# One metaformer layer on one core: the width transform, the filters and the mixing in tiles of 64 rows by 128 columns

## The chip, the core and the metric

The kernel runs on one core of a Trainium2 chip. A core has TensorE (PE: matrix products into PSUM, with weight loads of their own, PEld), VectorE (DVE), ScalarE (ACT), GpSimd (POOL) and SyncE (SP), each with its own queue of instructions in a fixed order, and 16 DMA engines that all queues share. PSUM has eight banks of 128 x 512 float32. The metric is the device time of one execution in microseconds; times are compared as medians of several executions.

## The reference

The input x is 8 images of 128 x 128 pixels with 96 channels, all float32. The layer computes, for each image:

```python
z  = layernorm_over_channels(x)
p  = relu(z @ w1.T) ** 2                       # 192 channels (scale 1, bias 0 as parameters)
f  = rfft2(p)                                  # 128 x 65 complex, per channel
r  = softmax(mlp(mean(z), mean(relu(bn(z @ sp_w.T)))))      # 3 x 192 weights per image
c  = sum(r[s] * resized_filter[s] for s in range(3))        # complex, 128 x 65 x 192
x  = x + irfft2(f * c) @ w2.T                  # back to 96 channels
y  = q(relu(q(q8(layernorm(x)) @ q8(W1).T + b1))) ; out = x + q(q8(y) @ q8(W2).T + b2)
```

q8 rounds to an 8-bit float with 2 bits of mantissa (float8e5), q to a 16-bit one. The three learned filters are small (16x9, 8x4, 24x13) and are resized to 128x65 by cubic interpolation, which is a product with fixed matrices. The Fourier transforms are products with fixed cosine and sine matrices too.

## The kernel before

Each image passes three **streams** of work, for which the kernel has one function each.

*before* (stream "a") works on units of four image columns. It normalises, projects (line 825, `px`), rectifies and squares on ScalarE, transforms along the height (line 854, `py`), folds rows that mirror each other (line 866) and stores the result Y to DRAM. At the end of an image a short chain (`rate_v0` to `rate_n`) gives the softmax weights.

*spectrum* (stream "s") works on 33 groups `g` of four rows of the half-transformed image (the last ones have fewer). A group's 192 channels are handled as three parts `q` of 64; two rows `k` of it lie beside each other. Its steps:

- `load_y` and `load_t` (SP's queue) bring Y as `yt` and the stored, half-resized filters T as `tb`; `weigh` (line 1028, GpSimd) multiplies `tb` in place by the softmax weights.
- `along_w` (line 1038) transforms along the width. Its float32 products have 64 rows of weights (`yt`) and 64 columns of them, and stream the 65 columns of the constant F2. Four of them, one for each quarter of the 128 x 128 array, follow each other: two halves `i` of the rows and two `k` of the columns.
- `filters_of` (line 1055) makes the filters in the same way, streaming the 130 columns of RW.
- `copy_sr` (line 1071), `make` (1078), `times` (1084 and 1089) and `turn_back` (1098 and 1101) form the complex product on ScalarE, VectorE and GpSimd and leave it in `xf`.
- For each pair `p` of groups, `mix_low` and `mix` (line 1136, both through `mix_part`) multiply `xf` with w2, streaming 96 columns into `pv`. The upper half of the odd columns uses a negated copy, w2N. `mixed` (line 1155) copies one part of `pv` to a tile B, `combine` (lines 1169 and 1171) adds it to, or takes the rest of `pv` from it, giving V. `invert` (line 1177) transforms back along the width, `inverted` copies and `store_v` stores.

*after* (stream "c") works on blocks of 16 image columns in units of four. `load_v` (lines 1267 and 1268, SP's queue) brings x and V as `t` and `vin`; `last` (line 1273) transforms back along the height; `residual` and `measure` add and take statistics on VectorE. `quantise` normalises one column at a time to float8 in the tile z8, on ScalarE (line 1297) and for one column in eight on VectorE (line 1295); in the last image every second column goes to VectorE. `turn` (line 1302) transposes four columns by a product with an 8-bit identity; `turned` casts the result to float8, on ScalarE (line 1316), in the last image on VectorE (line 1314). `first` (1320), `accumulated` (1327), `biased` (1331), `hidden` (1340, partly 1338), `second` (1347), `put` (1358), `bias` (1362) and `add_up` (1365) are the two layers of the feed-forward network.

A float32 matmul shows in the profile as two records of MATMUL and two of LDWEIGHTS. Products of the line set that the planner calls QUARTER (`along_w`, `filters_of`, `mix_low`, `mix`) leave the array's full-size mode.

**The order of the work.** Nothing runs in the order in which it is written. Each step is entered with `at(...)`: a place in time, what it needs, and the PSUM banks that it takes. `in_order` (line 395) then plays a list schedule on five engines: among the steps that are able to run on an engine it takes the one with the lowest score, which is its place (from the tables WINDOWS and OFFSETS) plus PATIENCE times its delay, and for TensorE plus TURN if the step would change between quarter and full mode. Durations are the fixed table COST (line 157). Six of the eight PSUM banks are dealt out by this plan. The resulting order is written into all queues and holds as it is.

Of the kernel before, what the change touches and what calls it, by code (L numbers as in the profile page):

```python
# [43 lines left out]
MED = 192  # L44
# [11 lines left out]
NG = 31  # L56
# [4 lines left out]
QW = 4  # L61
NQ = WB // QW
# [6 lines left out]
    "a": ((-200.9, 193.5), (639.2, 783.6), (807.7, 922.4), (818.6, 80.5), (148.2, 908), (1102.5, 495.5), (1851.5, 145.6), (2347.7, 470.5)),  # L69
    "s": ((676.9, 253), (431.2, 1046), (911.9, 290.8), (986.6, 574), (-10.7, 261.5), (686.4, 714.9), (1669.9, 93.5), (1887.9, 399.6)),  # L70
    "c": ((1205.2, 777.7), (1178.4, 353), (1360.1, 364.5), (2329.6, 155.8), (2330.5, 482.5), (2472.9, 753.3), (2695.6, 163.1), (2430.1, 646.2)),
}
OFFSETS = {
    "a_context": 98.12,
    "a_fold": 75.91,
    "a_inverse": -202.76,
    "a_load_r": -32.82,
    "a_load_x": -65.67,
    "a_load_xT": 129.83,
    "a_measure": 6.73,  # L80
    "a_project": 64.92,
    "a_put": -0.36,
    "a_rate_e": -236.48,
    "a_rate_n": 287.05,
    "a_rate_p0": -429.86,
    "a_rate_p1": 10.66,
    "a_rate_p2": -69.53,
    "a_rate_v0": -132.22,
    "a_rate_v1": 71.89,
    "a_rate_v2": -99.13,  # L90
    "a_rate_v3": -109.42,
    "a_rectify": -39.91,
    "a_rest": 0.92,
    "a_root": -123.7,
    "a_scale": -16.84,
    "a_square": 71.92,
    "a_store_r": 43.88,
    "a_store_y": -293.45,
    "a_transform": -53,
    "a_variance": 83.26,  # L100
    "c_accumulated": -93.43,
    "c_add_up": -46.53,
    "c_bias": -6.84,
    "c_biased": -64.47,
    "c_first": 13.27,
    "c_hidden": -20.41,
    "c_hidden_2": -145.18,
    "c_hidden_v": -14.93,
    "c_inverse": -0.79,
    "c_last": -164.24,  # L110
    "c_load_v": 67,
    "c_measure": 187.47,
    "c_put8": 23.31,
    "c_quantise": 188.57,
    "c_quantise_v": 329.63,
    "c_residual": -27.11,
    "c_rest": -161.76,
    "c_root": 97.28,
    "c_second": -234.45,
    "c_store": 15.78,  # L120
    "c_turn8": -593.06,
    "c_turned8": 183.6,
    "c_turned8_v": 3.41,
    "c_variance": -133.82,
    "s_alone_t": 91.08,
    "s_alone_x": 250.65,
    "s_alone_z": 38.64,
    "s_along_w": -51.21,
    "s_combine": -13.92,
    "s_copy_sr": -135.74,  # L130
    "s_filters_of": 34.27,
    "s_invert": -8.66,
    "s_inverted": -204.05,
    "s_load_t": 114.08,
    "s_load_y": 112.07,
    "s_make": 78.5,
    "s_mix": 85.47,
    "s_mix_low": 17.63,
    "s_mixed": -265.36,
    "s_store_v": -66.27,  # L140
    "s_times": -169.22,
    "s_turn_back": 36.2,
    "s_weigh": 4.83,
}
WAIT, PATIENCE, TURN = (0, 0, 0, 0, 1.42), (1.06, 54.4, 7.19, 78.2, 48.3), 5100.78
# [52 lines left out]
    "c_turned8_v": (DVE, 0.68, 0),  # L198
    "c_hidden_v": (DVE, 0.6, 0),
# [40 lines left out]
SHARED = {"a_scale", "c_biased", "a_rate_n", "a_rate_v3"}  # L240
# [154 lines left out]
def in_order(ops):  # L395
# [5 lines left out]

    n = len(ops)
# [15 lines left out]
    quarter, shared = [k in QUARTER for k in kinds], [k in SHARED for k in kinds]  # L418

# [14 lines left out]
    while len(order) < n:  # L434
        for e in stale:
# [4 lines left out]
            for i in able[e]:  # L440
                if e == PE:
                    t = last[PE] - (MODES[2] if mode and quarter[i] else MODES[1] if mode != quarter[i] else MODES[0])
                elif e == ACT and queued[i]:
                    t = max(issue, begun + 0.05)
                else:
                    t = last[e] - OVERLAP[e]
                if e == ACT and issue > t:
                    t = issue
                t = max(t, ready[i])
                if ops[i].banks:  # L450
                    if len(open_banks) < ops[i].banks:
                        continue
                    t = max(t, open_banks[ops[i].banks - 1])
                found.append((t, i))
# [29 lines left out]
        if e == PE:  # L484
            mode = quarter[i]
        if moves[i] > 0:
# [28 lines left out]
def metaformer_kernel(ctx: ExitStack, tc: tile.TileContext, a: dict, out: bass.AP):  # L515
# [49 lines left out]
    ident8 = const.tile([128, 128], F8, name="ident8")  # L565
    ones = const.tile([128, 1], F32, name="ones")
# [15 lines left out]
    w2N = const.tile([128, 3, C], F32, name="w2N")  # L582
# [6 lines left out]
    def projection(sp):  # L589
# [3 lines left out]
        ident = sp.tile([128, 128], F32, name="ident")  # L593
# [32 lines left out]
        def others():  # L626
            for i in range(2):
                nc.sync.dma_start(out=w2C[64 * i : 64 * i + 64, :, :], in_=a["w2T"].rearrange("(q m) c -> m q c", q=3))
            nc.vector.tensor_scalar(w2N, w2C, -1.0, None, ALU.mult)
# [367 lines left out]
    def spectrum(b, t0, P):  # L997
# [17 lines left out]
        def load_t(g):  # L1015
            tb = kept["tb", g] = psp.tile([128, 2 * MED], F32, name="tb", tag="tb", bufs=3)
# [9 lines left out]
        def weigh(g):  # L1026
            p = slice(0, 128 if g <= NG else 64)
            nc.gpsimd.tensor_tensor(kept["tb", g][p, :], kept["tb", g][p, :], rates[b][p, :], ALU.mult)  # L1028

        def along_w(g):  # L1030
            halves = [bank("pz") for _ in range(2)]
            kept["pz", g] = halves
            for cs in range(2 if g <= NG else 1):
                for q in range(3):
                    for k in range(2):
                        for i in range(2):
                            rows, c = slice(64 * i, 64 * i + 64), 2 * q + (cs if i == 0 else 1 - cs)
                            nc.tensor.matmul(  # L1038
                                halves[i][64 * k : 64 * k + 64, c * L : (c + 1) * L],
                                lhsT=kept["yt", g][rows, cs, q, k, :],  # L1040
                                rhs=F2[rows, cs, :],
                                start=True,
                                stop=True,
                            )

        def filters_of(g):
            pf = kept["pf", g] = psz.tile([128, 2, 512], F32, name="pf", tag="pf")
            tb = kept.pop(("tb", g))

            for q in range(3):  # L1050
                for k in range(2):
                    m0 = k * MED + 64 * q
                    for s in range(2 if g <= NG else 1):
                        p = slice(64 * s, 64 * s + 64)
                        nc.tensor.matmul(  # L1055
                            pf[64 * k : 64 * k + 64, s, q * 2 * L : (q + 1) * 2 * L],
                            lhsT=tb[p, m0 : m0 + 64],
                            rhs=RW[p, :],
                            start=True,
                            stop=True,  # L1060
                        )
# [64 lines left out]
        def mix_part(p, columns):  # L1126

            for i in columns:
                for q in range(3):
                    for h in range(2):  # L1130
                        for r in range(2):
                            if i >= len(_columns(p, r)):
                                continue
                            g, k = _columns(p, r)[i]
                            half, rows = slice(64 * h, 64 * h + 64), slice(64 * r, 64 * r + 64)
                            nc.tensor.matmul(  # L1136
                                kept["pv", p, r][half, i * C : (i + 1) * C],
                                lhsT=kept["xf", g][rows, k, q, half],
                                rhs=(w2N if k == 1 and h == 1 else w2C)[rows, q, :],
# [12 lines left out]
        def mixed(p, r):  # L1152
            v = kept["B", p, r] = psp.tile([128, 2 * C], F32, name="B", tag=f"B{r}")
# [9 lines left out]
        def combine(p, r, cs):  # L1163
# [4 lines left out]
            if cs == 0:  # L1168
                nc.vector.tensor_tensor(v, a, b, ALU.add)
            else:  # L1170
                nc.vector.tensor_tensor(v, b, a, ALU.subtract)
# [320 lines left out]
```

## Time and profile before

| | us |
|---|---|
| median of 3 runs (2870.8 to 2886.89) | 2871.54 |
| the profiled execution | 2874.85 |
| its span, first to last instruction | 2873.1 |
| TensorE busy, matmul | 2450.5 |
| VectorE busy | 2305.3 |
| ScalarE busy | 2142.1 |
| GpSimd busy | 1696.3 |

A row of the profile names a line, an engine, an operation, what it writes and reads, the shape and the count, then busy time and the mean of one in ns. "<-" in a row of waits means "was released by". "issue" is time in which an engine waited for nothing that the profile shows. A matmul record has a modelled end: records overlap, so the busy time of a group of them is the union. A queue named "instruction" carries the instructions of an engine.

### The profile page before, as it was taken

The page shows a single profiled execution, that of the slowest core. Times are in us where ns is not written, and L with a number is a line of the kernel's source. Part 1 is how long each engine was busy: PE and PEld are TensorE (multiplying, and loading weights), DVE is VectorE, ACT ScalarE, POOL GpSimd, SP SyncE. Part 2 cuts the span into 40 slices and gives each one's busy share as a digit, 9 for nine tenths or more (in the row PEclk, how much of TensorE's full clock was granted, in tenths as well). Part 3 has the DMA queues.
Part 4 walks back from the last instruction along what each step waited for, and adds up shares of the span by engine and source line. Part 5 has one row for each costly group of instructions (what it writes and reads, how often), then busy time and mean ns, then how long its engine had stood idle before and what let it go on. Part 6 is the DMA issues. An engine that isn't in the chain of part 4 may idle for free.

```text
span 2873.1 us, 98792 instructions
## 1 busy us (share of the span) xinstructions
PE 2450.5 (85%) x40162; PEld 1787.2 (62%) x40162; DVE 2305.3 (80%) x5485; ACT 2142.1 (75%) x4332; POOL 1696.3 (59%) x2534
## 2 busy tenths in 40 slices
PE   5888888988898899999989899898988988788664
PEld 3456666666666666666666667666666665556443
DVE  5568777788878877898988888897887878788697
ACT  2355445687875868878888788787888988889776
POOL 3135544566665555657767656566666676668544
PEclk9789999999999999999999899999999999999775
DMA  7788878987889788789877788778676575655431
GB/s 212 211 278 257 246 229 235 273 238 215 225 238 267 230 230 254 217 267 277 257 221 206 228 240 247 209 225 232 201 215 197 170 229 157 184 163 170 149 110 45
DMA packets 786015, 621.67 MB, mean 216 GB/s; under 512 B 578548, under 2 KB 719916, under 8 KB 785536
## 3 DMA queue, kind: packets, MB, share of 16 engines
q1 hardware_dynamic: 697496, 464.33, 58.5%
q10 hardware_dynamic: 88064, 151.02, 14.7%
q8 instruction: 317, 5.19, 0.7%
q14 instruction: 138, 1.13, 0.1%
HBM read 407.03 MB, written 208.16 MB: 214 GB/s over the span
## 4 chain that ended last, share of the span: by engine, by line
PE 47%; ACT 17%; DVE 12%; issue 8%; DMA 5%; POOL 2%; SPq 1%; ACTq 1%; POOLq 0%; DVEq 0%
PE px L825 8%; PE pv L1136 7%; PE py L854 7%; PE pf L1055 5%; PE pz L1038 5%; ACT y L1327 5%; PE pg L1177 4%; ACT h L1340 4%; PE pk L1273 3%; PE po L1347 3%; PE ph L1320 3%; ACT z L1297 2%; DVE st L737 2%; DMA vin<-Vd 2%; DMA yt<-Yd 2%
## 5 line engine op out<-in xcount | busy, mean ns | idle before, releaser
L825 PE MATMUL px<-W1S,zT 97*128 97x240 f32 x2048 | 508.4, 385 | 48.5 <-DVE zT L812 15.9
L825 PEld LDWEIGHTS px<-W1S,zT 97*128 97x128 f32 x2048 | 393.4, 198 | 158.5 <-issue 34.3
L854 PE MATMUL py<-X,F 128*128 128x384 f32 x1024 | 446.1, 531 | 15.1 <-DVE yst L866 4.8
L1327 ACT CAST y<-ph 128x512 f16<-128x512 f32 x768 | 417.9, 603 | 45.1 <-PE ph L1320 35.7
L1098 POOL TENSOR_TENSOR xf<-t 128x390 f32<-128x390 f32 x256 | 232.4, 908 | 348.7 <-DVE t L1084 337.2
L836 ACT ACTIVATE rl<-px 128x480 f32<-128x480 f32 x512 | 291.1, 579 | 133.1 <-PE px L825 111.4
L1340 ACT ACTIVATE h<-y 128x1536 fp8e5<-128x1536 f16 (+1 forms) x256 | 371.6, 1452 | 22.1 <-DVE y L1331 20.8
L1297 ACT ACTIVATE z<-t,ln_m,ln_r 128x96 fp8e5<-128x96 f32 x848 | 363.0, 475 | 10.5 <-POOL ln_m L770 3.8
L1331 DVE TENSOR_TENSOR y<-y,b1q 128x1536 f16<-128x1536 f16 x256 | 308.3, 1205 | 77.8 <-ACT y L1327 77.1
L850 POOL TENSOR_TENSOR sacc<-sacc,rl 128x192 f32<-128x192 f32 x248 | 176.4, 711 | 303.3 <-ACT rl L836 290.8
L1136 PE MATMUL pv<-w2C,xf 64*64 64x96 f32 x9264 | 317.8, 250 | 41.4 <-issue 40.6
L866 DVE TENSOR_TENSOR yst<-py,yb 128x384 f32<-128x384 f32 x512 | 262.7, 546 | 91.6 <-PE py L854 27.7
L1028 POOL TENSOR_TENSOR tb<-tb,r 128x384 f32<-128x384 f32 (+1 forms) x264 | 296.4, 1123 | 46.3 <-DMA tb<-T 42.2
L1078 DVE TENSOR_TENSOR d<-pz,sr 128x390 f32<-128x390 f32 x512 | 265.1, 553 | 66.5 <-ACT sr L1071 65.7
L1136 PEld LDWEIGHTS pv<-w2C,xf 64*64 64x64 f32 x9264 | 287.9, 137 | 43.2 <-issue 39.0
L1055 PE MATMUL pf<-RW,tb 64*64 64x130 f32 x6240 | 253.5, 288 | 58.9 <-issue 24.9
L1320 PE MATMUL ph<-zT,W1q 96*128 96x512 fp8e5 x768 | 257.5, 415 | 38.6 <-DVE zT L1314 13.6
L1038 PE MATMUL pz<-F,yt 64*64 64x65 f32 x12480 | 257.3, 224 | 34.5 <-issue 23.2
L1084 DVE TENSOR_TENSOR t<-d,pf 128x780 f32<-128x780 f32 x256 | 245.1, 958 | 47.1 <-PE pf L1055 19.0
L1038 PEld LDWEIGHTS pz<-F,yt 64*64 64x64 f32 x12480 | 232.0, 138 | 67.8 <-issue 31.9
L1055 PEld LDWEIGHTS pf<-RW,tb 64*64 64x64 f32 x6240 | 189.5, 139 | 130.0 <-issue 58.9
L1347 PE MATMUL po<-W2q,h 128*128 128x96 fp8e5 x3072 | 194.0, 218 | 81.3 <-ACT h L1340 54.3
(129 smaller groups left out, 5085.8 us busy)
## 6 DMA issues: line engine op xcount, KB each, us to landing
yt<-Yd SPq DMA_DIRECT2D x1040, 96.0 KB
Yd<-yst ACTq DMA_DIRECT2D x256, 384.0 KB
xb<-in_xw SPq DMA_DIRECT2D x64, 768.0 KB
rB<-Rd SPq DMA_DIRECT2D x128, 384.0 KB
zT<-in_xT SPq DMA_DIRECT2D x128, 384.0 KB
tb<-T SPq DMA_DIRECT2D x256, 192.0 KB
Vd<-gst ACTq DMA_DIRECT2D x128, 384.0 KB
t<-in_x SPq DMA_DIRECT2D x64, 768.0 KB
```

The lines of the kernel that those rows point to most:

```text
L825: nc.tensor.matmul(px[:, i * (MED + SCTX) : (i + 1) * (MED + SCTX)], lhsT=zTs[(b * NU // 2 + u // 2) % NZT][:, QW * (u % 2) + i0 + i, :], ...
L836: nc.scalar.activation(kept["rl", u][:, i0 : i0 + 2, :].rearrange("h w m -> h (w m)"), kept.pop(("px", u, i0)), AF.Relu)
L854: nc.tensor.matmul(py, lhsT=F1, rhs=kept["X", u][:, i0 : i0 + 2, :].rearrange("h w m -> h (w m)"), start=True, stop=True)
L1028: nc.gpsimd.tensor_tensor(kept["tb", g][p, :], kept["tb", g][p, :], rates[b][p, :], ALU.mult)
L1038: nc.tensor.matmul(halves[i][64 * k : 64 * k + 64, c * L : (c + 1) * L], lhsT=kept["yt", g][rows, cs, q, k, :], rhs=F2[rows, cs, :], start ...
L1055: nc.tensor.matmul(pf[64 * k : 64 * k + 64, s, q * 2 * L : (q + 1) * 2 * L], lhsT=tb[p, m0 : m0 + 64], rhs=RW[p, :], start=True, stop=True,)
L1136: nc.tensor.matmul(kept["pv", p, r][half, i * C : (i + 1) * C], lhsT=kept["xf", g][rows, k, q, half], rhs=(w2N if k == 1 and h == 1 else w ...
L1297: nc.scalar.activation(z, t, AF.Identity, bias=m, scale=r, saturate=False)
L1320: nc.tensor.matmul(kept["ph", u, n], lhsT=W1q[:, n * 128 : (n + 1) * 128], rhs=kept["zT", u], start=True, stop=True)
L1327: nc.scalar.copy(kept["y", u][:, n, :], kept.pop(("ph", u, n)))
L1331: nc.vector.tensor_tensor(y, y, b1q, ALU.add)
L1340: nc.scalar.activation(h, y, AF.Relu, saturate=False)
```

## The change

The change has four parts.

1. `along_w`, `filters_of` and `mix_part` use weights of 64 rows and 128 columns. One product then covers both rows `k` of a group, or both halves `h`, so each function issues half as many. For this `weigh` writes its product to a new tile `tw` in another order (part `q` outside, row `k` inside). As w2N can't be used for half of the columns of a product, it is dropped; the sign goes into `combine`, which multiplies B by a column of +1 and -1 (`sides`) in a scalar_tensor_tensor.
2. `tb` has two buffers instead of three and is released by `weigh`, `tw` has two, B has one instead of two. The waits follow: `weigh` waits for `filters_of` two groups back, `mixed` and `mix_low` for `combine` of the pair before.
3. In the last two images (EXACT = 6) `quantise` runs on GpSimd for every column and writes float32 into `vin`, whose values are used up by then; `turn` transposes in float32 with a float32 identity, as step `turn32`; `turned` casts to float8 on VectorE. `load_v` waits for `turn32` two blocks back.
4. The planner knows that TensorE's instructions come in blocks of 256: INSTR counts those of each step, and a step that would cross into a block before PAGE (4.5 in its units) after the last crossing is held back in the plan. The tables WINDOWS and OFFSETS have new numbers throughout, and WAIT, PATIENCE and TURN too. COST keeps its numbers and gains two rows.

```diff
+EXACT = 6
...
-WAIT, PATIENCE, TURN = (0, 0, 0, 0, 1.42), (1.06, 54.4, 7.19, 78.2, 48.3), 5100.78
+WAIT, PATIENCE, TURN = (0, 0, 0, 0, 2.2), (1.22, 0.556, 94, 1.87, 44.4), 0.63
...
+    "c_turn32": (PE, 1.06, 0),
+    "c_quantise_p": (POOL, 0.26, 0),
...
-SHARED = {"a_scale", "c_biased", "a_rate_n", "a_rate_v3"}
+SHARED = {"a_scale", "c_biased", "a_rate_n", "a_rate_v3", "c_quantise_v", "c_hidden_v"}
+INSTR = {
+    "a_project": 8, "a_transform": 4, "a_rate_p0": 4, "a_rate_p1": 8, "a_rate_p2": 12, "s_along_w": 48,
+    "s_filters_of": 24, "s_mix_low": 48, "s_mix": 48, "s_invert": 4, "c_last": 4, "c_turn8": 8, "c_turn32": 16,
+    "c_first": 2, "c_second": 24, "_rows": 8, "_ends": 16, "_make_weights": 4,
+}
+PAGE = 4.5
...
+                if e == PE and count[i] + page >= 256:
+                    over = t + (took[i] - MODES[0]) * (256 - page) / count[i]
+                    t += max(0.0, turned + PAGE - over)
                 found.append((t, i))
...
-            nc.gpsimd.tensor_tensor(kept["tb", g][p, :], kept["tb", g][p, :], rates[b][p, :], ALU.mult)
+            tw = kept["tw", g] = psp.tile([128, 2 * MED], F32, name="tw", tag="tw")
+            tb, order = kept.pop(("tb", g)), "p (k q m) -> p k q m"
+            nc.gpsimd.tensor_tensor(
+                tw[p, :].rearrange("p (q k m) -> p k q m", q=3, k=2),
+                tb[p, :].rearrange(order, k=2, q=3),
+                rates[b][p, :].rearrange(order, k=2, q=3),
+                ALU.mult,
+            )
...
-                    for k in range(2):
-                        for i in range(2):
-                            rows, c = slice(64 * i, 64 * i + 64), 2 * q + (cs if i == 0 else 1 - cs)
-                            nc.tensor.matmul(
-                                halves[i][64 * k : 64 * k + 64, c * L : (c + 1) * L],
-                                lhsT=kept["yt", g][rows, cs, q, k, :],
+                    for i in range(2):
+                        rows, c = slice(64 * i, 64 * i + 64), 2 * q + (cs if i == 0 else 1 - cs)
                         nc.tensor.matmul(
+                            halves[i][:, c * L : (c + 1) * L],
+                            lhsT=kept["yt", g][rows, cs, q, :, :].rearrange("w k m -> w (k m)"),
+                            rhs=F2[rows, cs, :],
...
+                    nc.tensor.matmul(
+                        pf[:, s, q * 2 * L : (q + 1) * 2 * L],
+                        lhsT=tw[p, 128 * q : 128 * q + 128],
+                        rhs=RW[p, :],
...
                             nc.tensor.matmul(
-                                kept["pv", p, r][half, i * C : (i + 1) * C],
-                                lhsT=kept["xf", g][rows, k, q, half],
-                                rhs=(w2N if k == 1 and h == 1 else w2C)[rows, q, :],
+                                kept["pv", p, r][:, i * C : (i + 1) * C],
+                                lhsT=kept["xf", g][rows, k, q, :],
+                                rhs=w2C[rows, q, :],
...
-            v = kept["B", p, r] = psp.tile([128, 2 * C], F32, name="B", tag=f"B{r}")
+            v = kept["B", p, r] = psp.tile([128, 2 * C], F32, name="B", tag=f"B{r}", bufs=1)
...
-                nc.vector.tensor_tensor(v, a, b, ALU.add)
+                nc.vector.scalar_tensor_tensor(v, b, sides, a, ALU.mult, ALU.add)
             else:
-                nc.vector.tensor_tensor(v, b, a, ALU.subtract)
+                nc.vector.scalar_tensor_tensor(v, b, sides, a, ALU.mult, ALU.subtract)
...
-            return "quantise_v" if i % 8 == 7 or b == B - 1 and i % 2 == 1 else "quantise"
+            return "quantise_p" if b >= EXACT else "quantise_v" if i % 8 == 7 else "quantise"
...
+            if b >= EXACT:
+                nc.gpsimd.tensor_scalar(z, t, r, m, ALU.mult, ALU.add)
+                return
...
-                    rhs=ident8,
+                    rhs=ident if b >= EXACT else ident8,
...
-            if b == B - 1:
+            if b >= EXACT:
                 nc.vector.tensor_copy(kept["zT", u], pz, saturate=False)
...
-                after = [one("last", blk - 2, n) for n in range(NQ)] + [one("store", blk - 5)]
+                after = [one(k, blk - 2, n) for n in range(NQ) for k in ("last", "turn32")] + [one("store", blk - 5)]
```

## The prediction

> **What bounds the kernel now.** I read the busy shares and the chain of the page first, then the long middle stretch alone, then TensorE's own waits in it, then the order of time around one mixing step.
>
> ```profile
> PE 2450.5 (85%) x40162; PEld 1787.2 (62%) x40162; DVE 2305.3 (80%) x5485; ACT 2142.1 (75%) x4332; POOL 1696.3 (59%) x2534
> ...
> q8 instruction: 317, 5.19, 0.7%
> ...
> PE 47%; ACT 17%; DVE 12%; issue 8%; DMA 5%; POOL 2%; SPq 1%; ACTq 1%; POOLq 0%; DVEq 0%
> ```
>
> No engine is full, but TensorE and "issue" are 55% of the chain. The stretch 360 to 2520 (us, PE busy, PEld, DVE, ACT, POOL, clock, DMA share, GB/s):
>
> ```profile
> 360.00:2520.00 2160.00, 1922.45 (x33949) 1429.73 (x33948) 1784.63 (x4176) 1702.80 (x3477) 1348.41 (x1971) 0.96 0.78 227
> ```
>
> TensorE is busy 89% there. Who let it wait in that stretch:
>
> ```profile
> PE pv L1136 <- issue: 70.9, 38, 4.1
> PE pf L1055 <- issue: 22.5, 17, 4.2
> PE pz L1038 <- issue: 18.5, 11, 3.5
> PE po L1347 <- ACT h L1340: 16.8, 23, 2.1
> ```
>
> With three small rows (4.2, 3.3, 2.8) "issue" is 122 us. So TensorE's work and its missing instructions fill 2045 of 2160 us (95%), and all other engines together cost it 115 us. TensorE is the bound; what happens in lines 1038, 1055 and 1136 counts nearly in full.
>
> The order of time (start, length, what):
>
> ```profile
> 1509.46 0.71 PE L1136 MATMUL pv<-w2C,xf 64*64 64x96 f32 x11 [2.63 <-issue]
> ...
> 1522.66 0.93 PE L1038 MATMUL pz<-F,yt 64*64 64x65 f32 x48
> 1523.41 0.85 PE L1055 MATMUL pf<-RW,tb 64*64 64x130 f32 x24
> 1524.08 1.24 PE L1136 MATMUL pv<-w2C,xf 64*64 64x96 f32 x50
> ```
>
> A float32 matmul is two records. Four records, one per 64x64 quarter, run at once: a **round**. Start to start, line 1038 takes 0.75 us for 12 rounds and line 1055 0.67 for 6; single records give a median round of 58, 111 and 82 ns (65, 130 and 96 columns). The first line is a stall: mixing stands 2.63 us with nothing to wait for but instructions.
>
> [...]
>
> [...]
>
> ```profile
> L932 PEld LDWEIGHTS pm<-sc,fc1b x16: 106/108/109, 209.4 to 2343.0; 48*36 48x36 f32 x16
> L1038 PEld LDWEIGHTS pz<-F,yt x12480: 129/135/228, 235.6 to 2659.0; 64*64 64x64 f32 x199
> L1179 PEld LDWEIGHTS pg<-V,GL x16: 187/190/190, 494.7 to 2674.8; 128*128 128x128 f32 x16
> L1179 PE MATMUL pg<-V,GL x16: 244/260/275, 494.9 to 2674.9; 128*128 128x96 f32 x16
> 1519.20 0.36 PE L1179 MATMUL pg<-V,GL 128*128 128x96 f32 x2
> ```
>
> 36, 64, 128 columns: 108, 135, 190 ns, some 0.85 ns a column over a fixed part. The last two rows are the nearest thing to the new form: two short float32 passes with 128-column weights. The pair takes 0.36 us, the first alone 0.246: the second ends **0.11 us** later, although 96 columns stream in 0.08 (line 1136). The load paces it, not the stream.
>
> [...]
>
> ```profile
> 57.77 0.58 PE L675 MATMUL pt<-cw,rh 24*128 24x384 f32 x1
> 63.99 0.60 PE L675 MATMUL pt<-cw,rh 16*128 16x384 f32 x3
> ```
>
> One takes 0.58 with its load, three at once 0.60: loads of different row groups don't queue.
>
> **The change part by part.**
>
> *Tiles of 64x128.* A call covers both column halves, so calls halve (records: line 1038 12480 to 6240, 1055 6240 to 3120, 1136 12288 to 6144), but a round is now two records, and rounds stay 3120, 1560 and 3072. The streams are unchanged; the weight loads are twice as wide, so a round lasts at least the 111 ns of line 1179. Transform: 3120 x (111 - 58) = +165 us. Filters: 111 already, 0. Mixing: 3072 x (111 - 82) = +89. Together **+254 us**, 87% of it (10838 of 12480 records) between 360 and 2520: +221. Bounds: 0, if the wide load were hidden, which line 1179 speaks against; far more, if the two row groups' loads queued, which line 675 speaks against.
>
> *Instruction blocks.* TensorE issues 2 x 40162 = 80,300 instructions, afterwards 80,300 - 31,000 + 512 = 49,800: some 198 blocks for 317. A mixing round brought 8 instructions in 82 ns (a block in 2.6 us), then 4 in 111 (7.1 us). The longest stalls are about 4 us, so a block will arrive while the one before is used. I take 95% of 122 us away: **-116**, between -60 and -133 (the whole run's sum).
>
> *The middle stretch:* +221 - 116 = +105. With TensorE slower, the 115 us of waits on others shrink; I take 30%, -34. **+71.** *Before 360:* 6% of the rounds, +16, half hidden by 79 us of idle TensorE: **+8**.
>
> *Combining.* The minus sign leaves w2N and goes into line 1169/1171 as a scalar_tensor_tensor: 496 of 346 ns. The nearest row, line 971 with the same 128x192, has a median of 418: 0 to +36 us on VectorE (it has 17% idle)[...]. I take **+10**.
>
> *Buffers.* The weighted filters get their own tile (tw, 2), tb goes from 3 to 2 but is free after weigh: GpSimd's 264 instructions of 1.12 us stay, and its strided write costs 0 to 10% of 296 us on an engine 59% busy: 0. The load instructions are as many as before. B goes from 2 to 1: line 1155 on ScalarE and mix_low on TensorE now wait for the combining of p - 1; queued behind them are all of ScalarE's and TensorE's later work. Cover: 128 pairs in 2420 us are 19 us apart, combining ends some 3 us after mixing. 0; where mixings are bunched, up to 3 us each.
>
> *Batches 6 and 7 (EXACT).* 256 quantisations go to GpSimd: 176 leave ScalarE (x 475 = -84 us), 80 VectorE (x 684 = -55). GpSimd's price isn't shown for 96 columns; between 0.21 us (line 559, 16 columns) and 0.4 (a quarter of line 1098's 390-column 0.91 over its fixed part): I take 0.3, +77. Batch 6's 32 casts move from ScalarE (609) to VectorE (679). Turning in float32: 64 units, 8 passes of 110 ns for 4 of 56: +42 us on TensorE. z8 now lies in vin, so SP's load waits for the turning two blocks back, with filter and y loads behind it; blocks are some 20 us apart there, so 0. After 2700 VectorE is busiest (144 of 173) and loses 0.7 x 8 us a block less the 0 of its casts: -25. From 2330 to 2700 ScalarE is at 88% and TensorE at 81%; TensorE gets 17 + 21, ScalarE loses 73: +15. **-10** together.
>
> *The order.* Leaving a tiling mode cost 5100 in the old scores, 0.63 in the new. TensorE switches 576 times now; entering costs some 0.15 us (197 ns from the last full record's end to the first quarter record's, against 58). I take 40% more, 230 x 0.15 = **+35**, between -40 (its new moments fit the engines better) and +120 (the table still prices transform and mixing as narrow tiles).
>
> Sum: 71 + 8 + 10 - 10 + 35 = +114. The profiled execution took 2874.85 (span 2873.1, 1.75 around it), 3.3 above the median of the runs shown, 2871.54. So 2989 profiled, about **2985** as a median.
>
> **The rivals.**
> 1. *Wide loads hide* (0.07): the round stays at its stream. Then -116, -10, no fewer other waits: about 2760. For it: the load records of line 1136 overlap everything now. Against: there a load (64 columns) is no longer than its stream.
> 2. *Gain and loss cancel* (0.08): the order's waits fall by half and the engines' slack takes the rest: 2845 to 2900.
> 3. *The order misfits* (0.12): planned at 58 ns a round, executed at 111, TensorE arrives late at everything placed after it; the 115 us of waits double: 3080 to 3200.
> 4. *Row groups' loads queue* (0.03): 222 ns a round, 3120 x 164 + 1560 x 111 + 3072 x 140 = +1115: about 3850.
>
> The forecast itself (0.70) has 2905 to 3075. Faster ends where the round stays under about 75 ns for the transform and 90 for mixing.
>
> **How the numbers follow.** The range takes the forecast's own, half of case 2 and the foot of case 3: 2885 to 3090. This kernel's measurement can't tell less than about 1% from no change. Faster by more than that 0.07, within 0.08, slower 0.85.
>
> **What would show it.** Line of along_w: 24 records a group instead of 48, but a length of some 1.5 us for 0.93; mixing some 1.4 a half for 1.0; filters unchanged near 0.85. TensorE's "issue" waits under 20 us, q8 near 200 packets, PE busy above 92% in the middle. Combining at 350 to 420 ns, quantising on GpSimd near 0.3 us. I am wrong if a round of two wide records is much nearer 60 than 111 ns.

## The result, and the profile after

The changed kernel takes 2965.04 us (median of 4 runs, 2959.96 to 2968.79), the kernel before 2871.43 (4 runs, 2870.8 to 2886.89): a ratio of 1.031 with an interval of 1.027 to 1.035, so it is slower by 3.1%. Its profiled execution took 2965.69 us, its span 2963.9. The forecast was 2985, from 2885 to 3090.

The page of the changed kernel: busy shares, the queue of TensorE's instructions (packets, MB, share), and the chain.

```profile
PE 2701.0 (91%) x24914; PEld 2075.7 (70%) x24914; DVE 2333.0 (79%) x5438; ACT 2085.4 (70%) x4124; POOL 1801.3 (61%) x2790
...
q8 instruction: 198, 3.24, 0.5%
...
PE 55%; ACT 11%; DVE 8%; DMA 4%; POOL 3%; issue 2%; SPq 1%; ACTq 0%; POOLq 0%; DVEq 0%
```

TensorE has 38% fewer matmul records and 250.5 us more busy time. Its instructions arrive in 198 packets instead of 317, and "issue" falls from 8% of the chain to 2%. The middle stretch of the changed kernel (columns as before: us, PE, PEld, DVE, ACT, POOL, clock, DMA share, GB/s):

```profile
360.00:2520.00 2160.00, 2071.32 (x20162) 1615.01 (x20162) 1786.76 (x4142) 1685.25 (x3407) 1318.67 (x1951) 0.98 0.78 223
```

TensorE is busy 96% of it, instead of 89%. Its waits over the whole run of the changed kernel, longest sums first (us in total, times, longest):

```profile
PE po L1374 <- ACT h L1367: 65.2, 41, 5.6
PE px L847 <- DVE yst L888: 24.1, 9, 13.9
PE po L1374 <- DVE h L1365: 15.5, 8, 2.5
PE pf L1081 <- POOL xf L1124: 13.8, 17, 1.7
```

No row of them is "issue", which had 134 us in the whole run before. The order of time in the changed kernel (start, length, what):

```profile
1509.07 0.94 PE L1081 MATMUL pf<-RW,tw 64*128 64x130 f32 x12
1509.85 1.45 PE L1066 MATMUL pz<-F,yt 64*128 64x65 f32 x24
...
1513.68 1.58 PE L1160 MATMUL pv<-w2C,xf 64*128 64x96 f32 x24
```

The transform takes 1.45 us for 12 rounds of two records (0.93 before), a mixing half 1.58 (1.24), the filters 0.94 (0.85). Single records give a median of 111 to 112 ns from round to round on all three lines, whether 65, 96 or 130 columns stream.

Three groups of the changed kernel that the prediction priced (busy us, mean ns, idle before with its releaser):

```profile
L1193 DVE SCALAR_TENSOR_TENSOR V<-B,sides,pv 128x192 f32<-128x192 f32 x248 | 101.2, 408 | 104.1 <-ACT B L1179 86.9 <-ACT V L1185 16.9
L1319 POOL TENSOR_SCALAR vin<-t,ln_r,ln_m 128x96 f32<-128x96 f32 x256 | 118.5, 477 | 1.2
L1329 PE MATMUL pz<-ident,vin 128*96 128x128 f32 x512 | 74.5, 293 | 2.7 <-POOL vin L1319 2.2 <-DVE d L1104 0.3
```

And GpSimd's longest waits in the changed kernel; the third is new:

```profile
POOL sacc L872 <- ACT rl L858: 268.1, 115, 19.1
POOL xf L1124 <- DVE t L1110: 224.8, 105, 7.8
POOL tw L1052 <- PE pf L1081: 148.2, 73, 10.8
```

`weigh` now waits 148 us for the filters two groups back.

**Where the time went.** The span is TensorE's busy time plus its idle time. From 2450.5 + 422.6 it went to 2701.0 + 262.9 us: 250.5 more work, 159.7 less idling, 90.8 in all. By phases: 4 us before the first `along_w`, 67 from there to the last mixing, 20 in the tail after the last mixing (202 to 222). That much could be read without another run. It doesn't tell which part of the change is responsible, because the parts came together.

### The profile page after: what moved, and what is told of

The parts are those of the page before. It is cut to its first block, busy times and chain, and to the rows that moved or that the text cites. A ratio compares the mean times of both kernels' runs of the same rounds, so it can differ in the third digit from the quotient of the medians.

```text
span 2963.9 us, 68657 instructions
## 1 busy us (share of the span) xinstructions
PE 2701.0 (91%) x24914; PEld 2075.7 (70%) x24914; DVE 2333.0 (79%) x5438; ACT 2085.4 (70%) x4124; POOL 1801.3 (61%) x2790
## 3 DMA queue, kind: packets, MB, share of 16 engines
q8 instruction: 198, 3.24, 0.5%
## 4 chain that ended last, share of the span: by engine, by line
PE 55%; ACT 11%; DVE 8%; DMA 4%; POOL 3%; issue 2%; SPq 1%; ACTq 0%; POOLq 0%; DVEq 0%
PE pv L1160 10%; PE pz L1066 9%; PE px L847 8%; PE py L876 7%; PE pf L1081 5%; PE pk L1297 4%; PE pg L1201 4%; PE po L1374 3%; PE ph L1347 3%; ACT y L1354 3%; ACT h L1367 2%; DVE y L1358 2%; DMA yt<-Yd 2%; PE pz L1329 2%; ACT z L1324 1%
## 5 line engine op out<-in xcount | busy, mean ns | idle before, releaser
L1066 PE MATMUL pz<-F,yt 64*128 64x65 f32 x6240 | 411.2, 277 | 8.2 <-ACT rl L858 2.8
L1066 PEld LDWEIGHTS pz<-F,yt 64*128 64x128 f32 x6240 | 388.5, 193 | 41.6 <-issue 11.7
L1160 PE MATMUL pv<-w2C,xf 64*128 64x96 f32 x6144 | 405.0, 281 | 3.7 <-POOL xf L1127 2.4
L1358 DVE TENSOR_TENSOR y<-y,b1q 128x1536 f16<-128x1536 f16 x256 | 343.2, 1341 | 67.0 <-ACT y L1354 66.0
L1160 PEld LDWEIGHTS pv<-w2C,xf 64*128 64x128 f32 x6144 | 386.6, 196 | 10.8 <-POOL xf L1127 2.7
L1052 POOL TENSOR_TENSOR tw<-tb,r 128x384 f32<-128x384 f32 (+1 forms) x264 | 285.5, 1083 | 176.3 <-PE pf L1081 148.2
L1324 ACT ACTIVATE z<-t,ln_m,ln_r 128x96 fp8e5<-128x96 f32 x672 | 286.5, 470 | 8.8 <-DMA yt<-Yd 3.3
L1374 PEld LDWEIGHTS <-h 128*128 128x128 fp8e5 x3072 | 163.5, 103 | 160.2 <-ACT h L1367 99.5
L1081 PE MATMUL pf<-RW,tw 64*128 64x130 f32 x3120 | 252.9, 292 | 22.8 <-POOL xf L1124 13.8
L1081 PEld LDWEIGHTS pf<-RW,tw 64*128 64x128 f32 x3120 | 208.1, 193 | 91.2 <-issue 30.4
```

What stands on the lines that cost most here:

```text
L1052: nc.gpsimd.tensor_tensor(tw[p, :].rearrange("p (q k m) -> p k q m", q=3, k=2), tb[p, :].rearrange(order, k=2, q=3), rates[b][p, :].rearra ...
L1066: nc.tensor.matmul(halves[i][:, c * L : (c + 1) * L], lhsT=kept["yt", g][rows, cs, q, :, :].rearrange("w k m -> w (k m)"), rhs=F2[rows, cs ...
L1081: nc.tensor.matmul(pf[:, s, q * 2 * L : (q + 1) * 2 * L], lhsT=tw[p, 128 * q : 128 * q + 128], rhs=RW[p, :], start=True, stop=True,)
L1160: nc.tensor.matmul(kept["pv", p, r][:, i * C : (i + 1) * C], lhsT=kept["xf", g][rows, k, q, :], rhs=w2C[rows, q, :], start=(i == 0 and q = ...
L1324: nc.scalar.activation(z, t, AF.Identity, bias=m, scale=r, saturate=False)
L1358: nc.vector.tensor_tensor(y, y, b1q, ALU.add)
```

## The experiments

The two theories. **Load:** the wide load makes the rounds longer, the missing stalls pay back about half, and the rest of the change is nearly neutral. **Order:** the wide tiles cost little in the end; the new order, with its buffers and last images, is what costs 3%.

A word on how to compare. The list schedule plays the steps with their places, needs and fixed costs. A kernel that changes none of these gets exactly the order of its parent on every engine: that holds for four of the kernels below (narrow and filters-wide in the new order, transform-wide and mixing-wide in the old one). The others get a plan of their own from places that were chosen for another; they are marked "new plan".

All runs in one table: the ratio to the kernel before with its interval, and of the profiled execution the span, TensorE's busy and idle time, its "issue" waits, and its time at half clock. The last is worked out from the mean granted clock c as 2 x (1 - c) x span, since the clock records of the first two kernels hold full clock and half clock and nothing between (61 records of each before, 35 of each in the changed kernel); for the others the same is taken, so that theirs is an estimate.

| kernel | ratio | span | busy | idle | issue | half clock |
|---|---|---|---|---|---|---|
| before | 1 | 2873.1 | 2450.5 | 422.6 | 134 | 391 |
| changed | 1.031 (1.027 to 1.035) | 2963.9 | 2701.0 | 262.9 | 0 | 320 |
| e1 all wide, old places, new plan | 1.071 (1.066 to 1.076) | 3063.6 | 2735.0 | 328.6 | 0 | 460 |
| e2 all narrow, new order | 1.030 (1.025 to 1.034) | 2946.0 | 2505.1 | 440.9 | 125 | 412 |
| e3 filters wide, new order | 1.013 (1.007 to 1.020) | 2901.2 | 2514.8 | 386.4 | 76 | 331 |
| e4 old quantising, new plan | 1.033 (1.028 to 1.038) | 2941.7 | 2664.7 | 277.0 | 0 | 341 |
| e5 filters wide, new plan | 1.030 (1.026 to 1.033) | 2961.4 | 2535.9 | 425.5 | 49 | 462 |
| e6 transform wide, old order | 1.004 (1.001 to 1.007) | 2886.0 | 2596.1 | 289.9 | 23 | 300 |
| e7 mixing wide, old order | 0.987 (0.984 to 0.991) | 2844.5 | 2533.3 | 311.2 | 15 | 341 |
| e9 one B, new plan | 1.020 (1.015 to 1.025) | 2913.6 | 2473.5 | 440.1 | 101 | 425 |
| e10 buffers alone, new plan | 1.025 (1.021 to 1.030) | 2937.9 | 2481.0 | 456.9 | 54 | 417 |
| e11 weighed in place, new plan | 1.075 (1.071 to 1.079) | 3080.4 | 2781.6 | 298.8 | 2 | 419 |
| e12 block model, new plan | 1.020 (1.014 to 1.026) | 2915.5 | 2472.1 | 443.4 | 55 | 414 |

**e8: the load by itself.** Into the kernel before, six stretches of products were put before the first spectra, four of 12 pairs and two of 12 single products; their results aren't used. They differ in the weights' columns, and in whether two row halves, one, or all 128 rows are used.

```diff
+        for _ in range(12):
+            for o, w, m in pair(128):
+                nc.tensor.matmul(o, lhsT=w, rhs=m, start=True, stop=True)
...
+        for _ in range(12):
+            nc.tensor.matmul(z[:, 0, :L], lhsT=GL[lo, :], rhs=F2[lo, 0, :], start=True, stop=True)
```

> The kernel before with a block of products of its own at the end of the set-up, whose results are not used: pairs on two row halves with 32, 64, 96 and 128 columns of weights, 65 streamed, 12 pairs each (24 rounds), then 12 with one row half and 12 with all 128 rows, 128 columns. Load theory (0.83 ns a column plus 5, row halves side by side): rounds of 58, 58, 85, 111, 111 and 111 ns. Rival (the two halves' loads queue): 64, 116, 170, 222, then 111 and 111. If the stream alone set the pace: 58 throughout.

The order of time in this kernel (start, length, what):

```profile
116.15 2.81 PE L737 MATMUL pf<-F,GL 64*32 64x65 f32 x48
118.89 2.02 PE L740 MATMUL pf<-F,GL 64*64 64x65 f32 x48
120.84 2.26 PE L743 MATMUL pf<-F,GL 64*96 64x65 f32 x48
122.93 2.85 PE L746 MATMUL pf<-F,GL 64*128 64x65 f32 x48
125.61 2.84 PE L748 MATMUL pf<-F,GL 64*128 64x65 f32 x24
128.38 3.90 PE L750 MATMUL pf<-F,GL 128*128 128x65 f32 x24
```

Each row is 24 rounds (24 single passes in the last two) with the same 65 columns streaming. From the end of one round to that of the next there are 58 to 59 ns at 64 columns of weights, 85 at 96, 111 to 112 at 128. Two row halves together (the fourth row), one alone (the fifth) and all 128 rows (the sixth) take the same 111 to 112: row halves don't queue, and rows don't count. The 0.83 ns a column of the load theory is (111 - 58) / 64, from the rounds at 64 and 128 columns; the 85 ns at 96 lie on the same line. The first row, the first 0.65 us of the second and the last 2.1 us of the sixth ran at half clock: some 108 ns for 32 and for 64 columns, 213 for 128. So at half clock the wide round nearly doubles, from 111 or 112 to 213 ns, and 32 columns cost as much as 64, 108 ns, which fits the stream setting the pace there. At full clock the load theory's figures hold for 64, 96 and 128 columns; 32 columns ran at half clock only. Rivals 1 and 4 of the prediction fall here. The whole kernel took 2875.98 us, beside 2874.68.

**e2 and e3: narrow tiles, then only the filters wide, in the new order.** e2 keeps all of the change but the tiles: three products have 64 columns again. e3 makes the filters alone wide. Both have the order of the changed kernel. e2's edit, for one of the three (against the changed kernel):

```diff
-                    for i in range(2):
-                        rows, c = slice(64 * i, 64 * i + 64), 2 * q + (cs if i == 0 else 1 - cs)
-                        nc.tensor.matmul(
-                            halves[i][:, c * L : (c + 1) * L],
-                            lhsT=kept["yt", g][rows, cs, q, :, :].rearrange("w k m -> w (k m)"),
+                    for k in range(2):
+                        for i in range(2):
+                            rows, c = slice(64 * i, 64 * i + 64), 2 * q + (cs if i == 0 else 1 - cs)
+                            nc.tensor.matmul(
+                                halves[i][64 * k : 64 * k + 64, c * L : (c + 1) * L],
+                                lhsT=kept["yt", g][rows, cs, q, k, :],
```

> The changed kernel with its products back in tiles of 64 by 64 and everything else kept (the plan and with it the order of the steps is the same). Load theory: rounds back at 58, 111 and 82 ns, q8 near 318 packets, issue waits of 100 us or more again, time near 2850 (2810 to 2900). Order theory: it stays near the changed kernel's 2965 (2940 to 2990).

> As the one with narrow products in the new order, but with the filters' product (130 columns streamed, so the stream hides the wide load) in tiles of 64 by 128. Load theory: filters' round stays at 111 ns, 24 blocks fewer (q8 near 294), issue waits 20 to 35 us less than with all narrow, time 10 to 40 us below it. Order theory: no difference beyond 10 us.

The page and then TensorE's waits for instructions in e2:

```profile
PE 2505.1 (85%) x40418; PEld 1824.9 (62%) x40418; DVE 2339.4 (79%) x5438; ACT 2068.9 (70%) x4124; POOL 1822.8 (62%) x2790
...
q8 instruction: 318, 5.21, 0.7%
```

```profile
PE pv L1165 <- issue: 50.8, 28, 4.4
PE pz L1067 <- issue: 47.2, 23, 4.1
PE pf L1084 <- issue: 13.8, 9, 4.6
```

e2 took 2944.07 us, nearer to the order theory's figure than to the load theory's, a ratio of 1.030 against the changed kernel's 1.031, and their intervals overlap: at the same order the three wide tiles together cost nothing that these runs can tell. (The order is one that was planned with the wide tiles' counts of instructions; e6 and e7 below are the other way round, wide tiles in an order planned for narrow ones.) The load theory's gain is not there; the stalls are, as in the kernel before. From e2 to the changed kernel TensorE's work grows by 196 us and its idling falls by 178, of which 125 are instructions. e3 took 2901.19 us, 43 less than e2 beside it: the filters gain 1.5% when widened alone. Their rounds were 111 ns already, 24 packets go, and the waits for instructions fall from 125 to 76 us. The two others then add the 1.8% between e3 and the changed kernel, across two sets of runs.

**e6 and e7: the transform or the mixing wide in the old order.** Each changes one function of the kernel before (e7 with the sign in `combine`), and nothing of needs, places or costs. e6's edit is the one shown for e2, the other way round; e7's:

```diff
-                                kept["pv", p, r][half, i * C : (i + 1) * C],
-                                lhsT=kept["xf", g][rows, k, q, half],
-                                rhs=(w2N if k == 1 and h == 1 else w2C)[rows, q, :],
+                                kept["pv", p, r][:, i * C : (i + 1) * C],
+                                lhsT=kept["xf", g][rows, k, q, :],
+                                rhs=w2C[rows, q, :],
```

> The kernel before with only the transform along w in tiles of 64 by 128. Load theory: its round goes from 58 to 111 ns, 3120 x 53 = 165 us, some 50 us of issue waits go: ratio 1.03 to 1.05. Rival (out of step besides): 1.06 and over.

> The kernel before with only the mixing in tiles of 64 by 128 and the sign in combine. Load theory: round from 82 to 111 ns, 3072 x 29 = 89 us, 50 to 70 us of issue waits go, combining 60 ns dearer: ratio 1.005 to 1.02. Rival (out of step besides): 1.03 and over.

The page and TensorE's waits for instructions in e7:

```profile
PE 2533.3 (89%) x34018; PEld 1871.1 (66%) x34018; DVE 2336.8 (82%) x5486; ACT 2146.6 (75%) x4332; POOL 1698.4 (60%) x2534
...
q8 instruction: 269, 4.41, 0.7%
```

```profile
PE pf L1056 <- issue: 8.4, 7, 2.7
PE pz L1039 <- issue: 6.2, 7, 2.7
```

Both expectations were too high. 15% fewer packets (317 to 269) took away 83% (e6) and 89% (e7) of the stalls: they aren't in proportion to the packets, and one wide function takes away nearly as much of them as all three. e6: 146 us more work, 133 less idling. e7: 83 more, 111 less. **e7 is faster than both kernels: 2832.7 us**, 1.3% below the kernel before in one set of runs, little more than the 1% that the prediction held to be the least to be told; its combining costs 408 and 405 ns as in the changed kernel. Mixing is the cheaper of the two to widen, for it loses 29 ns a round where the transform loses 53. In both the load theory's rounds are there; what failed was the price of their repayment. The order theory holds for these two. Transform and mixing wide together in the old order weren't run.

**e1, e5, e10, e9: the buffers and their waits in the old places.** e1 has all three products wide, with `tw`, two `tb` and one B; e5 only the filters; e10 the same buffers with narrow filters; e9 only the single B. All four get a new plan, since their needs change. The edits of the needs, against the kernel before (e9 has only the last pair of lines, the same in the needs of `mix_low`, and one buffer for B):

```diff
-            at(t - 0.003, load_t, g, after=[one("filters_of", g - 3)] + filled)
-            at(t, weigh, g, after=[one("load_t", g), (("a", b), "rate_n")])
+            at(t - 0.003, load_t, g, after=[one("weigh", g - 2)] + filled)
+            at(t, weigh, g, after=[one("load_t", g), one("filters_of", g - 2), (("a", b), "rate_n")])
...
-                b_free = [one("combine", p - 2, r, cs) for cs in range(2)]
+                b_free = [one("combine", p - 1, r, cs) for cs in range(2)]
```

> The kernel before with all three products in tiles of 64 by 128 (tw, the sign in combine, B with one buffer, as in the change), but its own places, scores and quantising. Load theory (a 128-column float32 load paces every round at 111 ns): rounds of 111 ns for lines of transform, filters and mixing alike, TensorE's issue waits under 20 us, q8 near 195 packets, time near 2970 (2940 to 3010). Order theory (the new places and the parts of the last images cost the time, not the tiles): fewer blocks only help, 2780 to 2860.

> The kernel before with only the filters' product in tiles of 64 by 128 (with tw, tb and B as in the change). Load theory: round stays at 111 ns because 130 columns stream that long anyway, 24 blocks fewer, so 25 to 45 us gained: ratio to before 0.984 to 0.992, faster than both kernels. Rival (any change of lengths or buffers puts the old order out of step): ratio 1.00 to 1.02.

> The kernel before with B in one buffer and the waits of mixed and mix_low on the combining of the pair before; products narrow, no tw. If what made the filters' kernel slow is tw and tb (weigh waits for filters two groups back, with all of GpSimd's queue behind it): ratio 0.995 to 1.01. If it is B's waits, or that the plan is made anew at all: 1.02 to 1.035.

> The kernel with wide filters in the old order, but with the filters' product back at 64 by 64, reading tw: the needs and so the plan are the same, only the product differs. If the needs that come with tw and B cost the time: ratio 1.03 to 1.05 (the 24 blocks saved are back). If the wide product itself costs it: 1.00 to 1.01.

A wait of GpSimd in e10, and then one of TensorE, counted from 240 to 2660 us (16.3 us in the kernel before):

```profile
POOL tw L1030 <- PE pf L1062: 111.8, 63, 7.3
```

```profile
PE pf L1062 <- POOL xf L1105: 53.2, 37, 4.1
```

e5 missed: not 1 to 2% faster but 3.0% slower, more than the rival's 2% too. e10 shows that its wide product isn't to blame, for without it the ratio is 1.025, just under the range for the needs (1.03 to 1.05), the two kernels' intervals just overlapping. TensorE's records have the shapes of the kernel before, its instruction waits fall by 80 us, and yet it idles 34 us more. It waits 53 us for the spectra on GpSimd, which itself waits 112 us in `weigh`; but in e12, which has a new plan and the old buffers, the same wait of TensorE is 28 us, so that a part of it comes with the plan. e9 changes B's waits only, doesn't touch `weigh`, and still costs 2.0%, the foot of what was expected if B's waits or a new plan are to blame. e12 bears on which of these two it is. e1 is the worst of the four, 7.1%, slower than either theory allowed for: the rounds of 111 ns and the missing stalls came as the load theory has them, but the idling fell by 94 us only, and TensorE's work grew by 284.5, with 460 us at half clock. Wide tiles in places that don't suit them are worse than the changed kernel.

**e12: a new plan and nothing else.** The kernel before, its work, waits and places untouched; only the planner gets the block model, with counts for narrow tiles.

```diff
+                if e == PE and count[i] + page >= 256:
+                    over = t + (took[i] - MODES[0]) * (256 - page) / count[i]
+                    t += max(0.0, turned + PAGE - over)
```

> The kernel before with only the planner's model of instruction blocks added (counts of its narrow products: 96, 48, 96, 96), its places and scores kept. If the model spreads the products so that blocks arrive in time: issue waits from 133 to under 70 us, ratio 0.98 to 0.995. If the old places and the score of 5100 for leaving the mode keep them bunched: issue waits over 100 us, ratio 0.995 to 1.03.

The model does what it is made for: instruction waits fall from 134 to 55 us. The time rises by 2.0% all the same, since other idling grows by 99 us and TensorE's busy time by 22: with the same work and the same waits. So a plan that is made anew can cost 2% by itself, and the whole of e9's loss is of that size. Whether it is the old places that don't suit the new plan, or the model's holding back of steps, isn't told apart. The expected gain missed; the other range, up to 3% slower, holds.

**e4 and e11: the last images' quantising, and weighing in place, in the new order.** e4 sets `EXACT` to 8 and puts back the old rule for `quantise` and `turned`. e11 takes away `tw` and goes back to three `tb`, weighed in place, with narrow filters. Both get a new plan. The first diff is e4's, the second e11's, both against the changed kernel.

```diff
-EXACT = 6
+EXACT = 8
...
-            return "quantise_p" if b >= EXACT else "quantise_v" if i % 8 == 7 else "quantise"
+            return "quantise_v" if i % 8 == 7 or b == B - 1 and i % 2 == 1 else "quantise"
```

```diff
-            at(t - 0.003, load_t, g, after=[one("weigh", g - 2)] + filled)
-            at(t, weigh, g, after=[one("load_t", g), one("filters_of", g - 2), (("a", b), "rate_n")])
+            at(t - 0.003, load_t, g, after=[one("filters_of", g - 3)] + filled)
+            at(t, weigh, g, after=[one("load_t", g), (("a", b), "rate_n")])
```

> The changed kernel with the last two images quantised and turned as before (8 bits, on ScalarE and VectorE); the plan is made anew with these steps. Theory that the float32 turning (some 42 us of TensorE) and GpSimd's 0.48 us per column lengthen the end: the stretch from the last mixing to the end falls from 222 to about 200 us, time near 2945 (2925 to 2960). Rival (the part costs nothing, ScalarE's relief pays for it): 2960 to 3000.

> The changed kernel with tb weighed in place in three buffers, no tw, and so with the filters' product at 64 by 64; transform and mixing stay wide, places and scores stay new. If weigh's wait for the filters costs time in the new order too: ratio to before 1.00 to 1.015. If the new places have made room for it: 1.025 to 1.04. GpSimd's wait of tw for pf, 148 us in the changed kernel, is gone in both cases.

e4 took 2952.73 us, a ratio of 1.033 beside 1.031: no difference that these runs can tell. The time lies in the range of the first theory (2925 to 2960), but its sign is missing. The tail after the last mixing is 225 us long without the new quantising, where about 200 were expected, 222 with it and 202 before, so its 20 us aren't explained by quantising on GpSimd. e2 and e3 have 224 and 225, the kernels in the old places 200 to 205, but e11, in the new places, 207. What makes the tail long isn't settled.

e11 missed by far: `weigh`'s wait of 148 us is gone, as meant, and the kernel is 4.2% slower than the changed one. It can't tell what the wait costs, since its plan is a new one too.

## Why the prediction was right, and where its sum was not

The time, the sign and the cause of the longer rounds were right. The sum had +114 us; the spans show +90.8. That it came so near is in part luck: the tiles were put at +79 us, and at the same order they cost 18; all the rest was put at +35 and cost 72.9. The two errors have opposite signs.

- **Rounds** (+254): right. 111 to 112 ns on all three lines, by the load, as e8 shows; the filters' busy time is unchanged (253.5 before, 252.9 after). From e2 to the changed kernel the transform's line grows from 261.7 to 411.2 us, that of mixing from 322.7 to 405.0 and that of the filters from 249.3 to 252.9, 235 us together.
- **Instruction blocks** (-116 of 122 us in the middle): right, 198 packets as worked out, and the stalls gone altogether. A packet is a block: 16.4 KB each (5.19 MB in 317, 3.24 in 198), and the traces hold 81,126 of TensorE's instructions before and 50,843 after, its semaphore waits among them, 256 and 257 to a packet. That a block comes while the one before is in use was the author's estimate; what is shown is that the waits are gone. What the step had no idea of is how early they go: e6 and e7 lose most of them with two fifths of that step's reduction (48 packets of 119).
- **"I take 30%, -34"** for the other waits: about right as a difference from the kernel before (115 to 89 us in the middle), too small at the same order, where from e2 to the changed kernel the idling beyond instructions falls by 53 over the whole run.
- **Missing from the sum: TensorE's clock.** From e2 to the changed kernel the three lines grow by 235 us, but TensorE as a whole by 196 only: its other lines, with the same instructions in the same order, took some 40 us less. With the clock records of the two traces laid over the matmul records, TensorE worked 322 us at half clock in e2 and 258 in the changed kernel, its other lines alone 262 and 177. Half of these differences is 32 and 42 us, an estimate that takes half-clock work to last twice as long (in e8 111.5 ns became 213). By it the clock accounts for what the other lines saved, and for 32 of the 58 us between 196 and the 254 of the rounds; 26 stay open. Why the clock was full for longer isn't shown. Fewer stalls for instructions don't bring it by themselves: e1 has none and 460 us at half clock.
- So **the middle stretch's +71 and the +8 before 360**, 79 in all, were the price of the tiles; at the same order the spans differ by 18 us (2946.0 to 2963.9). Rival 2 (gain and loss cancel, 2845 to 2900 us) missed the total, but at the same order gain and loss of the tiles did nearly cancel.
- **The order's +35:** the failed step. Together with combining, buffers and quantising the prediction had 35 us for all that is not tiles; e2 has exactly these parts, and shows 72.9. Its reason fails too: TensorE goes 576 times between the three lines and the others after the change, as before, where 40% more were taken. The price of entering was near: in the trace of before the first round of the three lines ends 198, 252 or 223 ns after the last full-size record where no wait lies between, 140 or 141 more than their rounds of 58, 111 and 82.
- **Buffers at 0:** `weigh` itself takes what it took, a median of 1001 ns for 1003, where 0 to 10% more was the author's estimate. Its wait was not named; it is 148 us on GpSimd, and TensorE's wait for the spectra that follow it is small (13.8 us) in the changed kernel. What it costs in time is open. In the old places e10 and e9 cost 2.5 and 2.0%, of which e12 can account for most.
- **Combining:** 408 and 406 ns against 350 and 342: 248 x (58 + 64) = 30 us of VectorE, near the upper bound of 36, for which 10 were taken; the lower bound of 0 was the author's estimate. e7 carries it and is faster than before.
- **Batches 6 and 7 (-10):** turning took 39.7 us more of TensorE (112.9 to 78.1 + 74.5; 42 were worked out), ScalarE's quantising 76.5 less (84), but one quantisation on GpSimd 477 ns, 119 us in all, for 0.3 and 77: the value lay above both ends of the estimate. Not foreseen was that VectorE's `biased`, which nothing in the change touches, took 343 us for 308; with the old quantising (e4) it is 316. Why isn't shown. In time, e4 finds no difference.
- **Rival 3** (TensorE late at everything) doesn't hold: its idling fell in every kernel with wide tiles whose order was kept.

What stays open is how the 2 to 3% of e2 divide between places, needs and last images. Taking any of them out makes a new plan, and a new plan by itself moved the time by 2% in e12.

## What to carry to other kernels

Price a tile by the longer of its load and its stream, per round, as these float32 products were paced (111 to 112 ns with 128 columns of weights, whether 65, 96 or 130 stream; 58, 82 and 111 with 64), then ask separately how few of the instructions have to go before most of the stalls stop: here 15% was enough, so the best kernel that was run widens one function, mixing, whose 82 ns a round are nearer to the wide load's 111 than the transform's 58, and leaves the rest (2833 us, 0.9 to 1.6% faster than before). Where the order of work is a plan made from chosen places, a change of needs or of the model counts as a change of the whole plan: try the arithmetic at the old order first, and compare only kernels of one order. A gain in the wait that a planner's model is written for, such as 79 us fewer instruction stalls here, says nothing on the sum of all waits.

## What was not expected of the hardware

- Stalls for instructions fall much faster than the instructions: 134 us with 317 packets, 23 and 15 with 269, none with 198. The order counts too: with 316 and 317 packets e10 and e12 have 54 and 55 us.
- TensorE worked at half clock for 239 us (e6) to 381 us (e1) of a run, by the traces' clock records (321 us before, 258 in the changed kernel). If all its work lasts twice as long there, as e8's rounds nearly did (58 and 108 ns, 111.5 and 213), it is longer by half of that, an estimate of 120 to 190 us, and the share changes with the order and with the tiles.
- In e8 the rounds become twice as fast at about 119.9 us and drop back to half that pace at about 130.1; the trace's own clock record has a spell of full clock from 119.8 to 130.0. At this place the record can be taken at its word.
- In e8 a float32 weight load of 128 columns sets 111 to 112 ns a pass at full clock, whether 64 rows, two times 64 or 128 are loaded.
